# Normalising attention once per query tile: the softmax sums of eight head groups packed on rows of one PSUM block

## The chip, the cores and the metric

The kernel runs on one core of one Trainium2 chip. Its time is the device time of one launch, in microseconds. The kernel before was timed in three runs: 1523.5, 1524.84 and 1529.5 us, median 1524.84 us. One further execution was recorded by the profiler; it took 1528.72 us, of which 1527.0 us lie between its first and its last instruction (the span).

## The reference

The input is `x` of shape 2 x 1024 x 1024 in fp32. One "macaron" block is applied: half a feed-forward step, attention, half a feed-forward step again, with the same feed-forward weights both times.

```
x = x + 0.5 * ffn(layernorm(x))
x = x + attn(layernorm(x))
x = x + 0.5 * ffn(layernorm(x))

ffn(x)  = x @ base_w.T + base_b + 2 * (top-2-of-8 gated LoRA, rank 16)
attn(x): q = x @ Wq (32 heads of 32), k, v = x @ Wk, x @ Wv (8 heads of 32), rotary embedding on q and k,
         att = q k^T / sqrt(32), causal; probs = softmax(att); ctx = probs @ v; out = ctx @ Wo
```

Four query heads share one key/value head. A *group* below is one key/value head with its four query heads; there are eight groups. What the change touches is the division by the sum in the softmax, after `probs @ v`.

## The kernel before

The 2048 rows are 16 query tiles of 128 rows, tiles 0 to 7 for the first sequence and 8 to 15 for the second. Each tile goes through four stages: `a1` (layernorm, first feed-forward), `a2` (q, k, v projections with rotary embedding), `c1` (output projection and third layernorm) and `c2` (second feed-forward). Between a2 and c1 lies the attention of the tile, in eight *units*, one per group. A large fp32 product is made of three fp16 matmuls, high x high, high x low and low x high, so each operand is kept as a high and a low part (`Split`, lines 297 to 326, with the two-buffer tile `hl` and the four-buffer tile `tt`).

A unit has two passes over the key blocks of its tile (1 to 8 blocks, since attention is causal; L is their number). `unit_s1` (lines 558 to 604) computes the scores with queries on the rows, and VectorE takes their maxima (line 590). The maxima are written into extra columns of the query tensor (lines 602 and 603), and a transposing DMA brings the queries back (`qt_load`, line 553). `unit_s2` (lines 704 to 725) computes the scores again, transposed, with keys on the rows; ScalarE takes the exponential (line 718). The result `p32` is multiplied with the values by `av_batch` (lines 639 to 675), in batches of at most four key blocks.

`av_batch` issues fp32 matmuls of 32 columns of weights, four of them side by side in the array, one for each query head of the group, so that head h lands on rows 32h to 32h+31 of the PSUM bank `av`. The first half of the bank, `av[:, 0]`, takes values times probabilities; the second half, `av[:, 1]`, takes a weight block of ones times the same probabilities (added in pairs by VectorE, line 636), which gives the softmax sum, repeated on the 32 rows of each head. After the last batch of a unit, these lines run, once per unit, 128 times in all:

```
nc.scalar.copy(o, av)                                   # line 664, ScalarE, 128x256
nc.vector.reciprocal(rc, rc)                            # line 666, VectorE, 128x128
nc.vector.tensor_tensor(o2, o[:, 0, :], rc, ALU.mult)   # line 671, VectorE
nc.scalar.copy(c.high(g), o2)                           # line 672, ScalarE, fp16 high part
nc.gpsimd.tensor_tensor(c.low(g), o2, c.high(g), ...)   # line 673, GpSimd, fp16 low part
```

`c.high(g)` and `c.low(g)` are blocks of the context tile `tt`, which is the stationary operand of c1: block g of the contraction of c1 is group g. There is one `av` bank (pool `p_av`, one buffer).

The order of the work is written out by hand: `plan` (line 870) gives for each step s the pieces of a1, a2, c1 and c2 that are run between the units of tile s, and `SEQS` (line 861) the exceptions. In most steps c1 of the tile before begins after three pieces of c2 and one of a2. Tile 8 (`LATE`) is attended last, after tile 15; in that last step c1 of tile 15 and c1 of tile 8 follow closely upon their attention. On top of that the Tile scheduler, with a timing model of its own, sets the order of the instructions on each engine. The DMAs go out from SP's queue in one order: weight streams (`ws<-wstr`, line 370), query transposes (line 553), layernorm transposes (line 314), key transposes (line 501), rows in and out. A DMA that waits on SP holds all that is behind it.

Of the kernel before, what the change touches and what calls it, by code (L numbers as in the profile page):

```python
# [9 lines left out]
FP = mybir.dt.float32  # L10
HP = mybir.dt.float16
I32 = mybir.dt.int32
AF = mybir.ActivationFunctionType
ALU = mybir.AluOpType
AX = mybir.AxisListType

B, T, D = 2, 1024, 1024
NH, NKV, DH, GRP = 32, 8, 32, 4
E, R = 8, 16
P = 128  # L20
KB = D // P
NT = B * T // P
TPB = T // P
# [16 lines left out]
def kernel(  # L40
# [16 lines left out]
    nc = tc.nc  # L57
# [3 lines left out]
    const = ctx.enter_context(tc.tile_pool(name="const", bufs=1))  # L61
# [4 lines left out]
    hlp = ctx.enter_context(tc.tile_pool(name="hl", bufs=2))  # L66
    tp = ctx.enter_context(tc.tile_pool(name="tp", bufs=4))
    dram = ctx.enter_context(tc.tile_pool(name="dram", bufs=1, space=bass.MemoryType.DRAM))
# [6 lines left out]
    p_av = ctx.enter_context(tc.tile_pool(name="p_av", bufs=1, space=bass.MemoryType.PSUM))  # L75
# [10 lines left out]
        out=cmask, in_=cmask, compare_op=ALU.is_ge, fill=-NEG, base=0,  # L86
# [6 lines left out]
        out=tri, in_=tri, compare_op=ALU.is_gt, fill=0.0, base=0,  # L93
# [3 lines left out]
    nc.gpsimd.memset(mhalf, -0.5)  # L97
    half = const.tile([P, 1], FP)
    nc.gpsimd.memset(half, 0.5)
    ones = const.tile([P, DH], FP)  # L100
    nc.gpsimd.memset(ones, 1.0)
    cosT = const.tile([P, TPB, DH // 2], FP)
    sinT = const.tile([P, TPB, DH], FP)
    bb = const.tile([P, D], FP)
# [192 lines left out]
    class Split:  # L297


        def __init__(self, n):  # L300
            self.hl = hlp.tile([P, 2 * D], HP, name="hl")
            self.tt = tp.tile([P, 2 * KB, P], HP, name="tt")
            self.n, self.done = n, 0
# [16 lines left out]
        def high(self, k):  # L320
            m = KB // self.n
            return self.tt[:, k // m * 2 * m + k % m, :]
# [163 lines left out]
    KT, VA, QS, CTX, CT = {}, {}, {}, {}, {}  # L486
# [119 lines left out]
    pend = deque()  # L606
    ready = {}
    avt = [None]

    class Context:  # L610


        def __init__(self):
            self.tt = tp.tile([P, 2 * KB, P], HP, name="tt")

        def high(self, k):
            return self.tt[:, k, :]
# [4 lines left out]
    pairs = {}  # L622

    def add_pairs(batch):

        t, g, L, us = batch
        key = (t, g, us[0][0])
        if key in pairs:
            return
        pairs[key] = []  # L630
        for i in range(0, len(us), 2):
            if i + 1 == len(us):
                pairs[key].append(us[i][1])
                continue
            sums = pp.tile([P, GRP, P], FP, name="pair", bufs=2)
            nc.vector.tensor_tensor(sums, us[i][1], us[i + 1][1], ALU.add)  # L636
            pairs[key].append(sums)

    def av_batch():

        add_pairs(pend[0])
        t, g, L, us = pend.popleft()
        if us[0][0] == 0:
            avt[0] = p_av.tile([P, 2, P], FP, name="av")
        av = avt[0]
        last = us[-1][0] == L - 1
        runs = [(0, VA[t - t % TPB + j][:, g, :], p32) for j, p32 in reversed(us)]
        runs += [(1, ones, sums) for sums in reversed(pairs.pop((t, g, us[0][0])))]
        prev = None
        for n, (i, w, p32) in enumerate(runs):  # L650
            for h in range(GRP):
                rows = slice(h * DH, (h + 1) * DH)
                with ExitStack() as st:
                    if prev is not None:
                        st.enter_context(tc.high_priority())
                        st.enter_context(tc.issue_after(prev.ins))
                    prev = nc.tensor.matmul(  # L657
                        av[rows, i, :], lhsT=w, rhs=p32[:, h, :],
                        start=(us[0][0] == 0 and n == 0), stop=(last and n == len(runs) - 1),
                        skip_group_check=True, tile_position=(0, h * DH),  # L660
                    )
        if last:
            o = pp.tile([P, 2, P], FP, name="o", bufs=2)
            nc.scalar.copy(o, av)  # L664
            rc = o[:, 1, :]
            nc.vector.reciprocal(rc, rc)  # L666
            if t not in CTX:
                CTX[t] = Context()
            c = CTX[t]
            o2 = pp.tile([P, P], FP, name="o2", bufs=1)  # L670
            nc.vector.tensor_tensor(o2, o[:, 0, :], rc, ALU.mult)
            nc.scalar.copy(c.high(g), o2)  # L672
            nc.gpsimd.tensor_tensor(c.low(g), o2, c.high(g), ALU.subtract)  # L673
            if g == NKV - 1:
                CT[t] = CTX.pop(t)

    def av_add(t, g, j, L, p32):

        if not pend or len(pend[-1][3]) == BATCH or pend[-1][0:2] != (t, g):
            pend.append((t, g, L, []))  # L680
        pend[-1][3].append((j, p32))
        after = 0
        while len(pend) > 1:
            after = sum(len(b[3]) for b in list(pend)[1:])
            add_pairs(pend[0])
            if after < SKEW:
                break
            av_batch()
# [38 lines left out]
    def stage_c1(t):  # L727
        while t not in CT:
            av_batch()
        tt = CT.pop(t)  # L730
        xt = xts[t]
        for n in range(2):
            ps = p_dense.tile([P, 512], FP, name="pd")
            yield from dense_streamed(ps, tt, 3 + n)
            c = bass.ts(n, 512)
            nc.vector.scalar_tensor_tensor(xt[:, c], ps, S["uo", n], xt[:, c], ALU.mult, ALU.add)
            if n == 0:
                yield True
        Ts["x3", t] = layernorm(xt)
        yield True  # L740
# [31 lines left out]
    for h in range(2):  # L772
        for src, c in ((a_in, slice(0, P)), (g_in, slice(P, P + E))):
            pin(
                nc.sync.dma_start(
                    out=agst[:, h, :, c],
                    in_=src[h * (D // 2) : (h + 1) * (D // 2), :].rearrange("(k p) n -> p k n", p=P),
# [57 lines left out]
    pp = ctx.enter_context(tc.tile_pool(name="pp", bufs=2, reuse_waits="tile"))  # L835
# [5 lines left out]
    def flush(_):  # L841
        while pend:
            av_batch()
        yield True
# [195 lines left out]
```

## Time and profile before

| What | us | Where it is read |
|---|---|---|
| median of three runs | 1524.84 | times |
| profiled execution | 1528.72 | times |
| span of that execution | 1527.0 | head of the page |
| TensorE matmul busy | 1404.1 (92%) | part 1 |
| VectorE busy | 1139.7 (75%) | part 1 |
| ScalarE busy | 755.5 (49%) | part 1 |
| GpSimd busy | 450.1 (29%) | part 1 |
| share of the chain that ended last: PE, DVE, DMA, ACT | 65%, 13%, 13%, 3% | part 4 |

The profile names engines PE (TensorE), DVE (VectorE), ACT (ScalarE), POOL (GpSimd) and SP (the queue that issues most DMAs). A row of a group gives the line, the engine, the operation, output and inputs with shapes and the count; after the first bar the total busy time in us and the mean of one in ns; after the second bar the time that the engine stood idle just before them, and what ended it. The matmuls are pipelined: one of 512 columns is shown as 0.38 us long, but they start 0.216 us apart, so busy time of PE is not work of PE. The chain of waits goes back from the last instruction, at each step to what released it.

### The profile page before, as it was taken

To read this page: it belongs to the slowest core of one execution; us is meant where nothing else is said; L and a number is where in the kernel's file an instruction comes from. 1 tells how busy PE (TensorE), PEld (TensorE's weight loads), DVE (VectorE), ACT (ScalarE), POOL (GpSimd) and SP (SyncE) were. 2 spreads that over 40 slices of the span, in tenths; PEclk is the share of its full clock that TensorE was granted. 3 is DMA by queue.
4 is the path that set the end of the run, shared out by engine and by line. 5 is a ranking of instruction groups with operands and counts; after the bars stand their busy time and mean duration, and the time that the engine had idled before them with its cause. 6 is when DMAs were issued, how large, how long until landed. Compare 5 with 4: busy or idle time off the path is not lost.

```text
span 1527.0 us, 35303 instructions
## 1 busy us (share of the span) xinstructions
PE 1404.1 (92%) x14548; PEld 783.4 (51%) x14548; DVE 1139.7 (75%) x2420; ACT 755.5 (49%) x1374; POOL 450.1 (29%) x665
## 2 busy tenths in 40 slices
PE   3686897989999999999999899999999999989998
PEld 2243444455555555555654445555555555556544
DVE  6877656686968879789764767886869788689753
ACT  7564334453545545456552434553545455556631
POOL 3443213432323233122121323332323232312231
PEclk9798999989999999999999999999999999999999
DMA  9957697658575581853646769857383853834651
GB/s 274 333 156 204 115 237 205 206 127 264 123 238 137 153 254 31 235 160 69 209 160 191 216 161 272 202 160 234 72 294 69 237 147 70 271 69 98 133 170 45
DMA packets 293075, 267.30 MB, mean 175 GB/s; under 512 B 258480, under 2 KB 261552, under 8 KB 272432
## 3 DMA queue, kind: packets, MB, share of 16 engines
q1 hardware_dynamic: 289360, 252.45, 60.5%
q10 hardware_dynamic: 3552, 12.58, 2.3%
q8 instruction: 114, 1.87, 0.5%
q14 instruction: 49, 0.40, 0.1%
HBM read 181.63 MB, written 20.45 MB: 132 GB/s over the span
## 4 chain that ended last, share of the span: by engine, by line
PE 65%; DVE 13%; DMA 13%; ACT 3%; issue 2%; POOL 1%; SPq 1%; DVEq 0%; ACTq 0%; POOLq 0%
PE pd L358 13%; PE pd L359 13%; PE pd L360 13%; PE av L657 10%; PE s L712 7%; PE s L573 6%; DMA ws<-wstr 6%; DMA qt<-qst 5%; DVE mx L590 3%; DVE pair L636 1%; DVE ws L195 1%; DMA tt<-hl 1%; DVE o L666 1%; ACT p L718 1%; DVE hl L311 1%
## 5 line engine op out<-in xcount | busy, mean ns | idle before, releaser
L718 ACT ACTIVATE p<-s,cs 128x512 f32<-128x512 f32 x576 | 382.3, 688 | 291.2 <-PE s L712 284.1
L590 DVE TENSOR_REDUCE mx<-s 128x4 f32<-128x512 f32 x480 | 313.6, 675 | 68.3 <-PE s L573 46.8
L358 PE MATMUL pd<-ws,tt 128*128 128x512 f16 x592 | 226.8, 383 | 20.9 <-DMA ws<-wstr 16.8
L636 DVE TENSOR_TENSOR pair<-p,p 128x512 f32<-128x512 f32 x256 | 185.6, 727 | 72.6 <-ACT p L718 34.8
L573 PE MATMUL s<-kts,qt 96*128 96x128 f16 x2304 | 217.0, 222 | 23.8 <-DMA qt<-qst 17.8
L359 PE MATMUL pd<-ws,tt 128*128 128x512 f16 x592 | 226.3, 382 | 0.0
L712 PE MATMUL s<-qt,kts 128*128 128x512 f16 x576 | 210.7, 386 | 16.4 <-DMA qt<-qst 11.6
L360 PE MATMUL pd<-ws,tt 128*128 128x512 f16 x592 | 225.4, 382 | 0.0
L573 PEld LDWEIGHTS <-qt 96*128 96x128 f16 x2304 | 165.5, 99 | 116.4 <-issue 30.4
L359 PEld LDWEIGHTS <-tt 128*128 128x128 f16 x1360 | 135.6, 100 | 141.9 <-issue 31.3
L358 PEld LDWEIGHTS <-tt 128*128 128x128 f16 x1360 | 135.6, 100 | 135.5 <-issue 16.7
L358 PE MATMUL pd<-wb,tt 128*128 128x512 f16 x512 | 199.0, 389 | 5.0 <-DVE xt L444 5.0
L360 PEld LDWEIGHTS <-tt 128*128 128x128 f16 x1360 | 135.3, 99 | 131.5 <-issue 10.2
L359 PE MATMUL pd<-wb,tt 128*128 128x512 f16 x512 | 198.0, 387 | 0.5 <-DVE wb L195 0.5
L360 PE MATMUL pd<-wb,tt 128*128 128x512 f16 x512 | 197.7, 386 | 0.0
L657 PE MATMUL av<-p,va 128*32 128x128 f32 x4608 | 166.8, 278 | 4.8 <-ACT o L664 2.5
L720 POOL TENSOR_SCALAR_AFFINE_SELECT p<-p 128x512 f32<-128x512 f32 x128 | 89.0, 698 | 274.7 <-ACT p L718 264.4
L673 POOL TENSOR_TENSOR tt<-o,tt 128x128 f16<-128x128 f32 x128 | 70.5, 551 | 279.6 <-ACT tt L672 279.3
L657 PEld LDWEIGHTS av<-p,va 128*32 128x32 f32 x4608 | 115.5, 110 | 68.3 <-issue 53.4
L666 DVE RECIPROCAL o<-o 128x128 f32<-128x128 f32 x128 | 120.6, 942 | 24.9 <-ACT o L664 24.9
L585 POOL TENSOR_SCALAR_AFFINE_SELECT sm<-sm 128x512 f32<-128x512 f32 x96 | 66.4, 692 | 203.9 <-ACT sm L584 202.1
L395 POOL TENSOR_TENSOR xt<-xt,bb 128x512 f32<-128x512 f32 x64 | 92.3, 1464 | 59.6 <-ACT xn L349 59.4
(177 smaller groups left out, 1808.2 us busy)
## 6 DMA issues: line engine op xcount, KB each, us to landing
ws<-wstr SPq DMA_DIRECT2D x148, 1024.0 KB, 5.9
wstr<-ws ACTq DMA_DIRECT2D x9, 1024.0 KB, 6.1
xt<-in_x_dram SPq DMA_DIRECT2D x16, 512.0 KB, 3.8
out_dram<-xt SPq DMA_DIRECT2D x15, 512.0 KB, 2.8
ws<-in_wb_dram SPq DMA_DIRECT2D x2, 1024.0 KB, 8.0
qst<-in_wb_dram SPq DMA_DIRECT2D x2, 1024.0 KB, 6.8
st<-in_wo_dram SPq DMA_DIRECT2D x2, 1024.0 KB, 10.0
kts<-in_wo_dram SPq DMA_DIRECT2D x2, 1024.0 KB, 12.0
```

Of the source, the lines that this page charges most:

```text
L358: nc.tensor.matmul(ps, lhsT=th, rhs=wh, start=(k == 0), stop=False)
L359: nc.tensor.matmul(ps, lhsT=th, rhs=wl, start=False, stop=False)
L360: nc.tensor.matmul(ps, lhsT=tl, rhs=wh, start=False, stop=(last and k == KB - 1))
L395: nc.gpsimd.tensor_tensor(xt[:, c], xt[:, c], bb[:, c], ALU.add)
L573: nc.tensor.matmul(ps[:, h, :], lhsT=q[0 : 3 * DH, h, :], rhs=KT[b0 + j][0 : 3 * DH, g, :], start=(not pem or h == 0), stop=not pem,)
L590: nc.vector.tensor_reduce(mx[:, odd, j, :], ps, AX.X, ALU.max)
L636: nc.vector.tensor_tensor(sums, us[i][1], us[i + 1][1], ALU.add)
L657: prev = nc.tensor.matmul(av[rows, i, :], lhsT=w, rhs=p32[:, h, :], start=(us[0][0] == 0 and n == 0), stop=(last and n == len(runs) - 1), ...
L666: nc.vector.reciprocal(rc, rc)
L712: ins = nc.tensor.matmul(ps.rearrange("p h k -> p (h k)"), lhsT=KT[b0 + j][:, g, :], rhs=q.rearrange("p h k -> p (h k)"), start=True, stop ...
L718: nc.scalar.activation(p32, ps, AF.Exp, scale=cs)
L720: nc.gpsimd.affine_select(out=p32, in_=p32, compare_op=ALU.is_ge, fill=0.0, base=0, pattern=[[0, GRP], [1, P]], channel_multiplier=-1,)
```

## The change

The weight block `ones` becomes `pick`: 39 columns, zero but for columns 7 and 15 to 38. A window of 32 columns that begins at column 7 - g has ones in column g (from column 7) and in columns 8 + g to 31. The sums of group g are so accumulated on row g of each head's 32 rows, and all eight groups could share one 128x128 block (the ones in the later columns put positive numbers on rows 8 and beyond, which are not used). The bank `av` now holds three blocks of values, for three groups, and one block of sums. It is copied out by ScalarE after groups 2, 5 and 7: the values without division into the memory of the context tile (`c.raw`, seen as fp32), the sums into `den0`, `den1`, `den2`. After group 7 `finish` runs, once per tile: VectorE adds the three blocks and takes one reciprocal, the ScalarE queue writes it to DRAM, four DMAs from SP's queue read it back, each repeating one head's eight rows on 32 partitions, into a tile taken from the two buffers `hl`; then VectorE multiplies in two halves of 512 columns, ScalarE makes the high part and GpSimd the low part, in two halves each.

```
-    ones = const.tile([P, DH], FP)
-    nc.gpsimd.memset(ones, 1.0)
+    pick = const.tile([P, NKV - 1 + DH], FP)
+    nc.gpsimd.memset(pick, 0.0)
+    nc.gpsimd.memset(pick[:, NKV - 1 : NKV], 1.0)
+    nc.gpsimd.memset(pick[:, 2 * NKV - 1 :], 1.0)
...
+    HG, SLOTS = NKV // 2, 3
     class Context:
         def __init__(self):
             self.tt = tp.tile([P, 2 * KB, P], HP, name="tt")
+            self.raw = self.tt.bitcast(FP).rearrange("p k c -> p (k c)")
+            self.raw = self.raw.rearrange("p (g c) -> p g c", c=P)
+            self.dens = []
+        def finish(self):
+            rc = pp.tile([P, P], FP, name="rc", bufs=1)
+            nc.vector.tensor_tensor(rc, self.dens[0], self.dens[1], ALU.add)
+            nc.vector.tensor_tensor(rc, rc, self.dens[2], ALU.add)
+            nc.vector.reciprocal(rc, rc)
+            flat = dram.tile([P, P], FP, name="rcd", bufs=2)
+            nc.scalar.dma_start(out=flat, in_=rc)
+            bc = hlp.tile([P, 2 * D], HP, name="hl").bitcast(FP).rearrange("p (g q) -> p g q", q=P)
+            rows = flat.rearrange("(h d) q -> h d q", h=GRP)[:, 0:NKV, :]
+            for h in range(GRP):
+                nc.sync.dma_start(
+                    out=bc[h * DH : (h + 1) * DH],
+                    in_=rows[h].rearrange("g q -> (g q)").partition_broadcast(DH),
+                )
+            for i in range(2):
+                g = slice(i * HG, (i + 1) * HG)
+                nc.vector.tensor_tensor(bc[:, g], self.raw[:, g], bc[:, g], ALU.mult)
+            for i in range(2):
+                g = slice(i * HG, (i + 1) * HG)
+                hi, lo = self.tt[:, i * HG : (i + 1) * HG], self.tt[:, KB + i * HG : KB + (i + 1) * HG]
+                nc.scalar.copy(hi, bc[:, g])
+                nc.gpsimd.tensor_tensor(lo, bc[:, g], hi, ALU.subtract)
...
-        if us[0][0] == 0:
-            avt[0] = p_av.tile([P, 2, P], FP, name="av")
+        first, last = us[0][0] == 0, us[-1][0] == L - 1
+        slot = g % SLOTS
+        if first and slot == 0:
+            avt[0] = p_av.tile([P, SLOTS + 1, P], FP, name="av")
...
-        runs += [(1, ones, sums) for sums in reversed(pairs.pop((t, g, us[0][0])))]
+        one = pick[:, NKV - 1 - g : NKV - 1 - g + DH]
+        runs += [(SLOTS, one, sums) for sums in reversed(pairs.pop((t, g, us[0][0])))]
...
-        if last:
-            o = pp.tile([P, 2, P], FP, name="o", bufs=2)
-            nc.scalar.copy(o, av)
-            rc = o[:, 1, :]
-            nc.vector.reciprocal(rc, rc)
-            o2 = pp.tile([P, P], FP, name="o2", bufs=1)
-            nc.vector.tensor_tensor(o2, o[:, 0, :], rc, ALU.mult)
-            nc.scalar.copy(c.high(g), o2)
-            nc.gpsimd.tensor_tensor(c.low(g), o2, c.high(g), ALU.subtract)
-            if g == NKV - 1:
-                CT[t] = CTX.pop(t)
+        if last and (slot == SLOTS - 1 or g == NKV - 1):
+            with tc.high_priority():
+                nc.scalar.copy(c.raw[:, g - slot : g + 1], av[:, 0 : slot + 1])
+                den = pp.tile([P, P], FP, name=f"den{len(c.dens)}", bufs=1)
+                nc.scalar.copy(den, av[:, SLOTS])
+                c.dens.append(den)
+        if last and g == NKV - 1:
+            c.finish()
+            CT[t] = CTX.pop(t)
```

More of the change, by code (lines that the diff above doesn't have):

```diff
@@ L642, in av_batch @@
         t, g, L, us = pend.popleft()
-        if us[0][0] == 0:
-            avt[0] = p_av.tile([P, 2, P], FP, name="av")
+        if t not in CTX:
+            CTX[t] = Context()
+        c = CTX[t]
+        first, last = us[0][0] == 0, us[-1][0] == L - 1
+        slot = g % SLOTS
+        if first and slot == 0:
+            avt[0] = p_av.tile([P, SLOTS + 1, P], FP, name="av")
         av = avt[0]
-        last = us[-1][0] == L - 1
-        runs = [(0, VA[t - t % TPB + j][:, g, :], p32) for j, p32 in reversed(us)]
-        runs += [(1, ones, sums) for sums in reversed(pairs.pop((t, g, us[0][0])))]
+        one = pick[:, NKV - 1 - g : NKV - 1 - g + DH]
+        runs = [(slot, VA[t - t % TPB + j][:, g, :], p32) for j, p32 in reversed(us)]
+        nv = len(runs)
+        runs += [(SLOTS, one, sums) for sums in reversed(pairs.pop((t, g, us[0][0])))]
         prev = None
@@ L658, in av_batch @@
                         av[rows, i, :], lhsT=w, rhs=p32[:, h, :],
-                        start=(us[0][0] == 0 and n == 0), stop=(last and n == len(runs) - 1),
+                        start=(first and slot == 0 and n == 0), stop=(last and n in (nv - 1, len(runs) - 1)),
                         skip_group_check=True, tile_position=(0, h * DH),
                     )
-        if last:
-            o = pp.tile([P, 2, P], FP, name="o", bufs=2)
-            nc.scalar.copy(o, av)
-            rc = o[:, 1, :]
[L666 to L669, printed above, removed]
-            o2 = pp.tile([P, P], FP, name="o2", bufs=1)
-            nc.vector.tensor_tensor(o2, o[:, 0, :], rc, ALU.mult)
-            nc.scalar.copy(c.high(g), o2)
-            nc.gpsimd.tensor_tensor(c.low(g), o2, c.high(g), ALU.subtract)
-            if g == NKV - 1:
-                CT[t] = CTX.pop(t)
+        if last and (slot == SLOTS - 1 or g == NKV - 1):
[7 more added lines that the diff above has]
+            CT[t] = CTX.pop(t)
     def av_add(t, g, j, L, p32):
```

## The prediction

> **What bounds the kernel now.** I read the page's busy shares and its chain first, then the rows that the change touches, then what TensorE waits for, then the last 70 us as a timeline.
>
> ```profile
> PE 1404.1 (92%) x14548; PEld 783.4 (51%) x14548; DVE 1139.7 (75%) x2420; ACT 755.5 (49%) x1374; POOL 450.1 (29%) x665
> ...
> PE 65%; DVE 13%; DMA 13%; ACT 3%; issue 2%; POOL 1%; SPq 1%; DVEq 0%; ACTq 0%; POOLq 0%
> ...
> L666 DVE RECIPROCAL o<-o 128x128 f32<-128x128 f32 x128 | 120.6, 942 | 24.9 <-ACT o L664 24.9
> ```
>
> TensorE is the bound: two thirds of the chain, DVE and DMA about one eighth each. The reciprocal is the one large row that shrinks: 128 calls of 942 ns, a tenth of DVE. Summing the chain's list in 20 us slices, L666 stands on it with 19.5 us (24 pieces) and its product L671 with 5.3 us (17 pieces): 24.8 us in all.
>
> ```profile
> PE s L573 <- DMA qt<-qst: 17.8, 10, 5.7
> PE pd L358 <- DMA ws<-wstr: 16.8, 15, 2.2
> PE s L712 <- DMA qt<-qst: 11.6, 12, 2.1
> ...
> PE pd L358 <- DMA tt<-hl: 6.1, 5, 2.1
> PE s L573 <- DVE mx L590: 5.7, 15, 0.9
> ...
> PE s L712 <- ACT p L718: 4.3, 11, 1.2
> ```
>
> These are TensorE's waits (total, times, longest). Waits for DMAs add up to 52.3 us. Waits for DVE or ACT in the attention are small: with `pair` 2.7, `o` L664 2.5 and `o` L671 0.5 they come to 15.7 us. DVE is near its limit only in stretches, such as this one in tiles 12 and 13 (five and six key blocks):
>
> ```profile
> 1150.00:1200.00 50.00, 49.89 (x620) 29.40 (x618) 46.77 (x96) 28.98 (x53) 14.56 (x21) 1.00 0.37 74
> ```
>
> DVE (third figure) is busy 46.77 of 50 us.
>
> **What goes and what comes, by engine.** DVE loses 128 x (942 + 341) ns = 164.2 us. It gains 32 adds of 128x128 at 341 (L671's form) = 10.9, 16 reciprocals = 15.1, 32 products of 128x512 at 727 (L636's form) = 23.3. Net -115 us. ACT loses 47.7 (L664) + 38.0 (L672). It gains 48 copies of values (373 for 256 columns, L664; about 480 for 384, between it and 584 for 512, L584), 48 of sums at 0.27 (L436's form) and 32 casts at 0.61 (L508): 21 + 13 + 20 = 54. Net -32 us. POOL loses 70.5 (L673) and gains 32 x 1.46 (L395, a 128x512 two-input operation) = 46.8. TensorE is unchanged: as many matmuls, `pick` has 32 columns like `ones`. DMA gains 16 x (64 KB + 4 x 128 KB) = 9.4 MB beside 267 MB. The first memsets are hidden behind the loads of the start, some 0.3 us on POOL if not.
>
> **What the relief is worth.** Between 0 (the next arrival in each place is as late) and 24.8 us (all that the removed work holds on the chain). I take 14 us: near the 15.7 us that TensorE waits for DVE and ACT, below it for the part that does not come from this work, with some of the query transposes' 29.4 us (they wait for DVE's maxima) on top.
>
> **The new path at the end of a tile.** The old one is short: in the last unit ACT copies at 1488.3, and GpSimd ends the low part at 1490.9, 2.6 us. Block g of c1 also needed only group g. Now c1's first block needs group 7 and all of `finish`: ACT's two copies 0.37 + 0.27; DVE 0.34 + 0.34 + 0.94; the write; the four reads; the first product 0.73, cast 0.61, low part 1.46. The write of 64 KB has no row; `out_dram` lands in 2.8 us for 512 KB and 2.0 for 256, so 1.4 on their line, 1.7 with smaller runs (ends 1.4 and 2.8). For the reads the nearest row is the one other broadcast to partitions:
>
> ```profile
> bb<-in_bias_dram SPq DMA_DIRECT2D x1, 512.0 KB, 4.9
> ```
>
> The same bytes, 4 KB repeated on 128 partitions, 4.9 us. [...] I take 4.5 from the first issue to the last landing. The path is then 0.64 + 1.62 + 1.7 + 4.5 + 0.73 + 0.61 + 1.46 = 11.3 us, with the turns in seven queues 12 us (9 to 16).
>
> What covers it is the TensorE work between the tile's last `av` matmul and c1's first. I counted it in the order in which the changed kernel's matmuls are issued, at 0.216 us for 512 columns, 0.056 for a score matmul and 0.03 for an `av` one, which are the timeline's spacings. Twelve tiles have 17 us or more, so nothing shows; were that cover gone, each would cost up to 12. Tile 14 has 10.9 (1 us shows, or none). Tile 9 has 7.1 (it was 0.9, with the short path). Tile 15 has 6.1. Tile 8 ends its attention 5.7 us after c1 of tile 15 begins, and 11.0 us of matmuls follow. TensorE issues in order, so what is queued behind the wait, c1 itself, a2 of tile 11 or c2 of the last tiles, stands too: 4.9 us at tile 9, 5.9 at tile 15, about 1 at tile 8, 1 at tile 14.
>
> A stall also costs clock:
>
> ```profile
> 1487.74 0.40 PE L657 MATMUL av<-p,ones 128*32 128x128 f32 x8
> 1489.69 0.59 PE L358 MATMUL pd<-ws,tt 128*128 128x512 f16 x1 [1.55 <-DMA ws<-wstr]
> 1490.07 0.63 PE L359 MATMUL pd<-ws,tt 128*128 128x512 f16 x1
> 1490.50 0.63 PE L360 MATMUL pd<-ws,tt 128*128 128x512 f16 x1
> ```
>
> After a wait of 1.55 us the next matmuls start 0.43 us apart until 1492.6, half speed, 1.5 us lost. [...] The row decides: 1.5 us for each of the two long stalls (3 us[...]), none for the short ones at tiles 8 and 14, which the row would put at up to 3 more. Exposed in all 4.9 + 5.9 + 1 + 1 + 3 = 15.8; the 0.5 that tile 9 waited before goes: 15 us.
>
> **SP's queue.** Each tile puts four reads there. The first waits until the write has landed, 1.7 us after ACT issues it, and with four issues (1.3) SP is held 3.0 us, 48 in all. Behind it stand query transposes, weight streams and layernorm transposes, for which TensorE waits. Priced at the share of the chain that runs through DMA and SP, 14%: 7 us. Ends: 0 (SP has idled for DVE anyway: its query transposes waited 206.8 us for L603) and 20 (every tile delays a needed stream by over 1 us).
>
> **Smaller terms.** The one `av` bank is now freed by two copies, 0.75 us instead of 0.37, 48 times instead of 128; TensorE waited 2.5 us for it before. +1 (0 to 18, if each is exposed). DVE's product waits for the reads, and maxima and pair sums stand behind it. By the order on DVE, 1 to 22 us of other work lie between the reciprocal and the product, mostly 6 or more (8 us at 75% busy) against about 7 us for write and reads; short of it are tiles 3, 7 and 11, some 4 us of idle DVE each, mostly not on the path: +2 (0 to 8). One `hl` buffer is lent for about 8 us per tile while the layernorm uses two; the transposes behind are needed a step later: 0.
>
> **Sum.** -14 + 15 + 7 + 1 + 2 = +11 us, on the profiled 1528.7 gives 1539.7 (span 1527.0 + 11 = 1538). The profiled run lies 3.9 above the median, so against 1524.84: 1536.
>
> **Rivals.** (a) *The relief decides; faster.* The place is DVE in the tiles with five to eight key blocks. If the whole 24.8 us come back and the queue term is nil, 1524.8 - 24.8 + 18 = 1518; with tile 9 also covered (-6), 1512. It decides as soon as relief exceeds the costs: with the costs at 25 it needs all of it, with SP at 0 it needs 18. For it: DVE at 94% above. Against: TensorE is 49.89 of 50 busy in the same window. (b) *No change.* The path is 9 us long, the two stalls shrink to 2 and 3 us: 1524.8 + 11 - 9 = 1527. For it: quick landings of small transfers; against: three engines' queues on the way. (c) *SP becomes the bound after each tile.* The queue term is 20 and the path 16 us: 1536 + 13 + 8 = 1557. For it: 52.3 us of waits for DMA already; against: SP's own idle time. That the change doesn't act as it says I leave out: the DVE rows must shrink.
>
> **Chances and range.** Faster by over 0.5% (below 1517, rival a) 0.24; within 0.5%, which is about what timing this kernel can tell (1517 to 1532.5, rival b and the weak end of mine) 0.21; slower 0.55, of it 0.42 mine and 0.13 rival c. Range 1511 to 1557: it keeps most of a and c; my own case alone is 1530 to 1546.
>
> **What would show it.** DVE busy near 1025 us, L666's successor at 16 calls. TensorE waits of 4 to 7 us for GpSimd's or ACT's part of the context before c1 of tiles 9 and 15, followed by 0.43 us spacing; none at the other tiles. Waits for `qt` and `ws` up by about 7 us. The prediction is wrong if waits for `mx`, `p` and `pair` fall by more than 20 us, if the reads land within 3 us, or if a wait for the `av` copies appears 48 times.

## The result, and the profile after

The changed kernel takes 1539.26 us (median of 14 runs; 1523.57 us for the kernel before, 14 runs): a ratio of 1.0095, with a 95% interval of 1.0068 to 1.0123, so some 14.5 us slower. Its profiled execution took 1544.15 us, 15.4 more than that of before, with a span of 1542.4 us.

The page's busy times, its chain by engines, and the row of the reciprocal:

```profile
PE 1410.2 (91%) x14548; PEld 785.9 (51%) x14548; DVE 1055.0 (68%) x2244; ACT 723.5 (47%) x1246; POOL 422.9 (27%) x571
...
PE 62%; DVE 14%; DMA 13%; issue 4%; ACT 2%; POOL 2%; SPq 2%; DVEq 0%; POOLq 0%; ACTq 0%
...
L628 DVE RECIPROCAL rc<-rc 128x128 f32<-128x128 f32 x16 | 15.2, 947 | 0.2
```

The reciprocal shrinks from 120.6 us to 15.2, VectorE's busy time by 84.7 us and ScalarE's by 32.0, and TensorE is the bound as before. In the chain the share of TensorE falls by three points, and VectorE's, "issue" and SP's each rise by one or two.

TensorE's waits after (total us, times, longest), beside the eight shown of before:

```profile
PE s L576 <- DMA qt<-qst: 15.2, 8, 7.9
PE pd L361 <- ACT tt L644: 13.3, 4, 5.3
PE s L744 <- DMA qt<-qst: 13.2, 5, 4.5
PE pd L361 <- DMA ws<-wstr: 12.1, 10, 2.9
...
PE s L744 <- ACT p L750: 7.7, 13, 3.5
PE av L694 <- DVE pair L667: 5.6, 5, 2.4
...
PE s L576 <- DVE mx L593: 3.3, 12, 0.5
...
PE pd L361 <- DMA tt<-hl: 2.0, 3, 0.9
```

The waits for the query transposes are 28.4 us in their two rows (29.4 before), those for weight streams 12.1 (16.8). New is `ACT tt L644`, TensorE at c1 waiting for the high part that ScalarE makes of the normalised values: 13.3 us in four tiles. The waits for exponentials (`ACT p`) and for pair sums grew from 4.3 to 7.7 and from 2.7 to 5.6.

VectorE's waits have this new row, the product in `finish` waiting for the four reads:

```profile
DVE hl L640 <- DMA hl<-rcd: 37.5, 14, 6.2
```

and ScalarE's this one, the cast of the high part waiting for that product:

```profile
ACT tt L644 <- DVE hl L640: 48.8, 16, 6.3
```

The two transfers of the round trip (the last figure is the median from issue to landing):

```profile
hl<-rcd SPq DMA_DIRECT2D x64, 128.0 KB, 2.7
rcd<-rc ACTq DMA_DIRECT2D x16, 64.0 KB, 2.0
```

The stretch of 50 us in which VectorE was busy 46.77 us before:

```profile
1150.00:1200.00 50.00, 49.65 (x611) 29.32 (x610) 43.02 (x89) 30.08 (x51) 18.99 (x22) 1.00 0.47 106
```

VectorE has 43.02 there now, and TensorE 49.65 where it had 49.89.

Where those two waits go is seen in the timeline of the changed kernel at the end of tile 3 (start, duration, engine, line; in brackets the idle time before and what ended it):

```profile
415.06 0.94 DVE L628 RECIPROCAL rc<-rc 128x128 f32<-128x128 f32 x1
...
416.03 0.33 ACTq L630 DMA_DIRECT2D rcd<-rc  x1
...
416.46 1.84 ACT L750 ACTIVATE p<-s,cs 128x512 f32<-128x512 f32 x3 [3.16 <-DVE rc L628]
...
419.62 1.72 SPq L634 DMA_DIRECT2D hl<-rcd  x4
...
420.89 0.38 PE L744 MATMUL s<-qt,kts 128*128 128x512 f16 x1
...
421.97 0.38 PE L445 MATMUL pd<-lbh,ll 128*128 128x512 f16 x1
...
423.88 1.29 DVE L640 TENSOR_TENSOR hl<-tt,hl 128x512 f32<-128x512 f32 x2 [5.96 <-DMA hl<-rcd]
424.61 0.62 ACT L644 CAST tt<-hl 128x512 f16<-128x512 f32 x1 [6.30 <-DVE hl L640]
425.10 0.69 DVE L667 TENSOR_TENSOR pair<-p,p 128x512 f32<-128x512 f32 x1
425.13 0.68 ACT L750 ACTIVATE p<-s,cs 128x512 f32<-128x512 f32 x1
...
425.87 0.59 PE L744 MATMUL s<-qt,kts 128*128 128x512 f16 x1 [3.52 <-ACT p L750]
...
426.50 0.59 PE L361 MATMUL pd<-ws,tt 128*128 128x512 f16 x1
426.87 0.63 PE L362 MATMUL pd<-ws,tt 128*128 128x512 f16 x1
427.30 0.63 PE L363 MATMUL pd<-ws,tt 128*128 128x512 f16 x1
```

The reciprocal ends at 416.0, the write goes out at 416.03, the reads at 419.62, after the write has landed. VectorE finds 1.9 us of other work and then stands 5.96 us before the product. Behind the product stands the pair sum (425.10), although the exponentials that it adds had ended by 418.30. ScalarE's cast waits for the product, and behind the cast, in ScalarE's order, stands the exponential (425.13), although its scores had ended by 421.27. The second-pass scores of TensorE at 425.87 wait for that exponential, 3.52 us, and then matmuls of 512 columns start 0.43 us apart in place of 0.216 until 431.1, 12 of them at this half speed: 12 x 0.216 = 2.6 us more. So one wait of 5.96 us on VectorE stands ahead of 6.1 us lost on TensorE.

### The profile page after: what moved, and what is told of

It is laid out like the page before. It is cut to its first block, busy times and chain, and to the rows that moved or that the text cites. A ratio compares the mean times of both kernels' runs of the same rounds, so it can differ in the third digit from the quotient of the medians.

```text
span 1542.4 us, 35022 instructions
## 1 busy us (share of the span) xinstructions
PE 1410.2 (91%) x14548; PEld 785.9 (51%) x14548; DVE 1055.0 (68%) x2244; ACT 723.5 (47%) x1246; POOL 422.9 (27%) x571
## 4 chain that ended last, share of the span: by engine, by line
PE 62%; DVE 14%; DMA 13%; issue 4%; ACT 2%; POOL 2%; SPq 2%; DVEq 0%; POOLq 0%; ACTq 0%
PE pd L361 13%; PE pd L362 13%; PE pd L363 12%; PE av L694 10%; PE s L576 6%; PE s L744 6%; DMA qt<-qst 4%; DVE mx L593 4%; DMA ws<-wstr 3%; DMA hl<-rcd 3%; DVE pair L667 2%; DMA rcd<-rc 2%; DMA tt<-hl 1%; DVE ws L198 1%; SPq L634 1%
## 5 line engine op out<-in xcount | busy, mean ns | idle before, releaser
L593 DVE TENSOR_REDUCE mx<-s 128x4 f32<-128x512 f32 x480 | 315.0, 682 | 97.2 <-PE s L576 63.6
L361 PE MATMUL pd<-ws,tt 128*128 128x512 f16 x592 | 229.9, 388 | 27.0 <-ACT tt L644 13.3
L667 DVE TENSOR_TENSOR pair<-p,p 128x512 f32<-128x512 f32 x256 | 190.7, 747 | 67.7 <-ACT p L750 25.2
L576 PE MATMUL s<-kts,qt 96*128 96x128 f16 x2304 | 215.6, 221 | 18.8 <-DMA qt<-qst 15.2
L744 PE MATMUL s<-qt,kts 128*128 128x512 f16 x576 | 212.8, 387 | 21.7 <-DMA qt<-qst 13.2
L362 PE MATMUL pd<-ws,tt 128*128 128x512 f16 x592 | 229.9, 388 | 0.0
L363 PE MATMUL pd<-ws,tt 128*128 128x512 f16 x592 | 228.2, 386 | 0.0
L363 PEld LDWEIGHTS <-tt 128*128 128x128 f16 x1360 | 135.8, 100 | 131.6 <-issue 14.3
L588 POOL TENSOR_SCALAR_AFFINE_SELECT sm<-sm 128x512 f32<-128x512 f32 x96 | 70.9, 738 | 195.7 <-ACT sm L587 187.7
L352 ACT ACTIVATE xn<-xt,nb,rs 128x1024 f32<-128x1024 f32 x48 | 59.5, 1239 | 71.2 <-DVE nb L347 58.7
L694 PE MATMUL av<-pair,pick 128*32 128x128 f32 x2048 | 87.1, 276 | 5.8 <-DVE pair L667 5.6
```

The lines of the kernel that those rows point to most:

```text
L361: nc.tensor.matmul(ps, lhsT=th, rhs=wh, start=(k == 0), stop=False)
L362: nc.tensor.matmul(ps, lhsT=th, rhs=wl, start=False, stop=False)
L363: nc.tensor.matmul(ps, lhsT=tl, rhs=wh, start=False, stop=(last and k == KB - 1))
L576: nc.tensor.matmul(ps[:, h, :], lhsT=q[0 : 3 * DH, h, :], rhs=KT[b0 + j][0 : 3 * DH, g, :], start=(not pem or h == 0), stop=not pem,)
L588: nc.gpsimd.affine_select(out=sm, in_=sm, compare_op=ALU.is_ge, fill=-3.0e38, base=0, pattern=[[0, GRP], [-1, P]], channel_multiplier=1,)
L593: nc.vector.tensor_reduce(mx[:, odd, j, :], ps, AX.X, ALU.max)
```

## The experiments

In the table "us" is the ratio less one, times the 1523.6 us of the kernel before. The next three columns are from the profiled run of each: how long VectorE's product waited for the reads, how long TensorE waited in all, and how many of its matmuls of 512 columns that the timeline shows singly (about 4,100 in each) lasted over 0.5 us, those that run at half speed.

| Kernel | ratio (95%) | us | product's wait | TensorE's waits | at half speed | span |
|---|---|---|---|---|---|---|
| before | 1 | 0 | none | 117.5 | 95 | 1527.0 |
| changed | 1.0095 (1.0068-1.0123) | +14.5 | 37.5 | 127.4 | 145 | 1542.4 |
| before_no_recip | 0.9769 (.9748-.9791) | -35.2 | none | 90.4 | 82 | 1484.3 |
| after_no_reads | 0.9841 (.9816-.9866) | -24.2 | 0 | 97.2 | 70 | 1493.8 |
| after_late_product | 1.0000 (.9985-1.0016) | 0 | 25.3 | 114.2 | 113 | 1519.9 |
| after_short_path_4_tiles | 1.0123 (1.0099-1.0146) | +18.7 | 34.4 | 126.7 | 112 | 1537.8 |
| after_late_and_short_4 | 0.9928 (.9900-.9955) | -11.0 | 15.2 | 109.7 | 106 | 1514.2 |
| after_late_and_short_7 | 0.9888 (.9868-.9909) | -17.1 | 7.1 | 104.7 | 74 | 1503.9 |
| after_reads_on_act | 1.0171 (1.0137-1.0205) | +26.1 | 40.7 | 131.3 | 149 | 1551.7 |
| after_late_reads_on_act | 1.0063 (1.0035-1.0091) | +9.6 | 21.9 | 126.9 | 110 | 1536.0 |
| after_reads_on_gpsimd | 1.0096 (1.0071-1.0120) | +14.6 | 43.8 | 121.0 | 94 | 1529.4 |
| after_spread_on_tensor | 1.0067 (1.0045-1.0089) | +10.2 | 0 | 101.3 | 83 | 1530.4 |
| after_spread_tensor_late_4 | 0.9925 (.9906-.9944) | -11.4 | 0 | 91.0 | 66 | 1508.2 |

before_pow_on_gpsimd, at 2.15 times the time, is told below. The last columns add up: take from the span TensorE's waits and 0.216 us for each matmul at half speed, and what remains is 1376 to 1389 us in every kernel with the same TensorE work (before 1389, changed 1384, no reads 1381, late with short path in seven 1383). The spans lie 67 us apart, these remainders 13, so most of what differs between these kernels is TensorE's waiting and the clock after it. The profiled runs are single executions, those of before and changed some 5 us above their medians; the times are judged by the ratios.

**What the relief is worth.** The kernel before, without the reciprocal; its product takes a constant block, so the softmax is not divided by its sums.

```
-            rc = o[:, 1, :]
-            nc.vector.reciprocal(rc, rc)
+            rc = bb[:, 0:P]
```

> The kernel before with the reciprocal of line 666 left out (the product takes a constant block in its place, so the context is not normalised): 128 x 942 ns = 120.6 us less on VectorE, nothing else changed. The forecast's theory: the relief of VectorE is worth about 14 us (0 to 19.5, what L666 holds on the chain), so about 1510 us. The rival, that TensorE is the bound everywhere and the relief is worth nothing: 1520 to 1527 us.

Measured: 1486.55 us, 35.2 us faster, well over twice the 14 us of the theory, with VectorE's busy time down by 99.2 us (1139.7 to 1040.5): 0.35 us for each us of VectorE. TensorE's waits for DMAs in this kernel:

```profile
PE s L573 <- DMA qt<-qst: 10.4, 6, 5.2
PE s L711 <- DMA qt<-qst: 5.8, 6, 1.6
PE pd L358 <- DMA ws<-wstr: 16.3, 11, 2.8
```

The weight streams are as before (16.3 for 16.8), the query transposes 16.2 us for 29.4. These 13.2 us are nearly as much as all that TensorE waits for VectorE and ScalarE by name in the attention there (15.7): the transposes start when VectorE's maxima are done (in the kernel before, SP stood 206.8 us ahead of them, waiting for line 603), so a DMA's name on a wait can hide VectorE.

**The round trip as a whole.** The changed kernel with the write, but without the four reads; the product takes a constant block `cb`, so nothing is normalised.

```
-            for h in range(GRP):
-                nc.sync.dma_start(out=bc[h * DH : (h + 1) * DH], in_=rows[h]...)
+            cb = cst.unsqueeze(1).to_broadcast([P, HG, P])
...
-                nc.vector.tensor_tensor(bc[:, g], self.raw[:, g], bc[:, g], ALU.mult)
+                nc.vector.tensor_tensor(bc[:, g], self.raw[:, g], cb, ALU.mult)
```

> The changed kernel without the four reads of the reciprocals (the product takes a constant block, so the context is not normalised); the write to DRAM stays, and every other instruction too. The forecast's theory: the loss is all in the way through DRAM (TensorE's four waits for the context, VectorE's 37.5 us of waiting for the reads, SP's 44 us of waiting for the write) and the relief remains: about 1510 us, TensorE's wait for the context under 2 us. The rival, that the packed bank, its two copies out and the wider products and casts cost it: 1530 us or more.

Measured: 1495.96 us, 24.2 us faster than before. This is the relief that the change could bring; what comes with the reads costs 38.7 us on top of it, which makes the +14.5. The edit takes away a little more than the transfers: the product no longer needs the sums either, and in ten of the 16 tiles the trace shows both of its halves ahead of the tile's reciprocal (tile 3: 409.47 and 412.04 against 415.09). The run with TensorE in place of DRAM, below, keeps that dependence, and puts what the edit adds in this way at about 3 us. The same 22 us of the timeline, around the end of tile 3, as one window (TensorE's busy time first, the granted clock third from the end), in the changed kernel

```profile
410.00:432.00 22.00, 18.11 (x148) 8.64 (x141) 13.72 (x20) 8.51 (x17) 7.62 (x8) 0.84 0.53 117
```

and without the reads

```profile
410.00:432.00 22.00, 21.02 (x229) 11.37 (x228) 16.05 (x28) 10.87 (x20) 7.11 (x9) 1.00 0.54 153
```

show TensorE busy 18.11 us at a clock of 0.84 against 21.02 at 1.00.

**Which part of the round trip: the tile's end, the queue or the product?** Three edits, each taking one away.

(1) The short path of before, unit by unit, in the four tiles in which TensorE waited at c1 (0, 8, 9 and 15):

```
+    OLD = {0, LATE, LATE + 1, NT - 1}
...
+        own = t in OLD
+        slot = 0 if own else g % SLOTS
...
+        if last and own:
...
+            nc.scalar.copy(o, av[:, 0, :])
...
+            nc.scalar.copy(rc, av[:, SLOTS, :])
+            nc.vector.reciprocal(rc, rc)
...
+            nc.vector.tensor_tensor(o2, o, rc, ALU.mult)
+            nc.scalar.copy(c.high(g), o2)
+            nc.gpsimd.tensor_tensor(c.low(g), o2, c.high(g), ALU.subtract)
```

> The changed kernel, but tiles 0, 8, 9 and 15, whose context TensorE waited for, are normalised unit by unit as before. The forecast's theory (the exposed ends of these tiles are the largest cost): the 13.3 us of waits and some 3 us of half clock go, a quarter of the relief (3.5 us) is given back, so about 1527 us. The rival, that the queues behind the reads in all tiles are the cost: 1536 us or more.

Measured: 1539.47 us, where the theory had 1527 and its rival 1536 or more. None of the four waits at c1 is left, and nothing is won. VectorE's row says why in part:

```profile
DVE hl L643 <- DMA hl<-rcd: 34.4, 12, 6.6
```

The four tiles had 13.2 of the changed kernel's 37.5 us, but in the twelve that keep the round trip the waits are 34.4 us where they had been 24.3; tiles 10 and 11 alone have 10.1 us for 3.7. In these two VectorE had less other work between reciprocal and product (6.5 us for 10.5, 2.0 for 3.2); why the order came out so stays open. VectorE's busy time is also 24.9 us longer here, so the edit does more than take away the waits at c1.

(2) The product, and with it the casts and low parts that use it, later: in tiles 2 to 6 and 10 to 14 behind the pair sums of the next tile's first units. The transfers and their queues are the same. In the trace the product stands behind more work in eight of these tiles (3 to 6 and 11 to 14; in tile 3, 5.9 us for 2.0).

```
+        def apply(self, after=None):
...
+                with ExitStack() as st:
+                    if after is not None:
+                        st.enter_context(tc.issue_after(after))
+                    nc.vector.tensor_tensor(bc[:, g], self.raw[:, g], bc[:, g], ALU.mult)
...
+        elif first and g == NKV_AT:    # NKV_AT = 1
+            apply_all(pair_ins[-1] if pair_ins else None)
```

> The changed kernel with the product, and so the casts, of tiles 2 to 6 and 10 to 14 put later on VectorE: behind the pair sums of the next tile's first units. VectorE's wait for the reads in these tiles (19.5 us of 37.5) should nearly go. The forecast's theory prices these waits at 2 us: 1537 us. The rival, that the maxima and pair sums held behind the product are what costs the time: 1525 to 1530 us.

Measured: 1521.55 us, 14.5 us less than the changed kernel by the ratios and below the 1525 to 1530 of the rival. VectorE's row

```profile
DVE hl L652 <- DMA hl<-rcd: 25.3, 10, 6.8
```

fell by 12.2 us. Of TensorE's waits those at c1 did not fall at all, those for exponentials and pair sums did:

```profile
PE pd L361 <- ACT tt L656: 13.3, 4, 6.0
...
PE s L769 <- ACT p L775: 3.7, 11, 1.0
...
PE av L715 <- DVE pair L688: 1.5, 3, 1.0
```

These two fell by 8.1 us, from 7.7 and 5.6, and the 32 fewer matmuls at half speed are worth 6.9 us at 0.216: 15.0 in all, for 14.5 measured. TensorE's waits for DMAs stayed (42.0 us, 42.5 in the changed kernel), and SP still waited 44.4 us for the landing of the writes (44.1). So the place of the product, with its casts, in the engines' orders is what costs these 14.5 us, not the tile's end or SP's queue.

(3) The reads from another queue, so that SP does not stand behind the write: ScalarE's, as below, once with the product where it was and once with it late; and GpSimd's, by the same edit.

```
-                nc.sync.dma_start(
+                nc.scalar.dma_start(
```

> The changed kernel with the four reads issued from ScalarE's queue, right behind the write, and not from SP's. SP is no longer held by them (44 us in the changed kernel), nor do the reads stand behind weight streams on SP; ScalarE waits for the write instead, about 2 us per tile. The forecast's theory (SP's queue costs 7 us): about 1532 us. A stronger form of it (reads that land late because of what SP has issued before them are what VectorE waits for): 1520 to 1527 us, with VectorE's wait for the reads well under 20 us. The rival (it is the round trip as such): 1537 us or more, the wait for the reads unchanged.

> The late product with the reads on ScalarE's queue. If what the late product leaves (25 us above the kernel without reads) is SP's queue and late landings: about 1510 us. If it is the exposed ends of four tiles: 1518 us or more.

> The four reads of each tile go out from GpSimd's queue in place of SP's; nothing else. SP no longer stands 44 us behind the landing of the write; GpSimd (28% busy) does, with its selects and low parts behind. Theory (the hold of SP costs nothing, the wait of VectorE's product does): that wait stays at 30 us or more and the time stays within 1534 to 1548. Rival (SP's hold is a large part of the loss): 1520 to 1530, with TensorE's waits for qt and ws down by 5 us or more.

Measured: 1550.35 and 1535.21 us on ScalarE's queue, 11.6 and 9.6 us more than with SP's (26.1 against 14.5, and 9.6 against 0); the first fits its rival, the second only the outcome of 1518 or more. ScalarE's own work now stands behind the reads, and so in part behind the landing of the write:

```profile
ACT lg L401 <- DMA hl<-rcd: 7.4, 1, 7.4
ACT p L750 <- DMA hl<-rcd: 4.2, 1, 4.2
ACT tt L701 <- DMA hl<-rcd: 2.6, 1, 2.6
```

and TensorE's waits for exponentials rise from 7.7 to 14.3 us, and from 3.7 to 13.2 in the late form. On GpSimd's queue, 1535.16 us: the ratio is that of the changed kernel to 0.0001. TensorE's waits there:

```profile
PE s L576 <- DMA qt<-qst: 13.8, 9, 7.6
PE pd L361 <- DMA ws<-wstr: 12.5, 11, 3.1
PE s L744 <- DMA qt<-qst: 11.1, 7, 3.7
PE av L694 <- DVE pair L667: 10.7, 10, 3.8
PE av L694 <- POOL p L752: 8.4, 7, 3.4
```

Those for transposes and weights are 37.4 us where the changed kernel has 40.5, those for pair sums and GpSimd's masked exponentials 19.1 for 11.0. GpSimd waited 23.0 us for the write in SP's place. So freeing SP gave nothing in the time that the hold of another queue did not take back. What SP's hold costs is not shown by this: TensorE's waits for DMAs are 42.5 us in the changed kernel, 38.9 with the reads on GpSimd's queue, 35.9 on ScalarE's, and 34.7 without reads.

**The two together.** Late product, with the short path in tiles 0, 8, 9 and 15:

> The late product together with the unit-by-unit normalisation of tiles 0, 8, 9 and 15. If TensorE's 13.3 us of waits for the context in those four tiles count in full, with the half clock behind two of them: 16 us less than the late product alone, and some 8 us back for VectorE's additional work (29 us at the price that the kernel before without the reciprocal shows, 0.3 us per us): about 1513 us. If the ends do not count: 1522 us or more.

Measured: 1510.51 us, 11.0 us faster than before, near the 1513 for ends that count. The product's wait:

```profile
DVE hl L655 <- DMA hl<-rcd: 15.2, 7, 3.7
```

Then the three tiles in which it had still waited longest (1, 7 and 10; 9.4 us) on the short path too, seven in all:

```
-    OLD = {0, LATE, LATE + 1, NT - 1}
+    OLD = {0, 1, LATE - 1, LATE, LATE + 1, LATE + 2, NT - 1}
```

> The late product, with the short path in seven tiles (0, 1, 7, 8, 9, 10, 15) in place of four: the three added are those where the product waited longest, 3.4, 2.3 and 3.7 us. Theory: 9.4 us of waits go at 1 to 1.5 us each, and three tiles of relief at 25.5/16 = 1.6 us each are given back: 1510.5 - 9 to 14 + 5 = 1502 to 1506. Rival (a late product already hides these waits): 1511 to 1516.

Measured: 1505.39 us, within the theory's 1502 to 1506, 17.1 us faster than before with an interval of 0.9868 to 0.9909, and the fastest of all in which nothing is left out. Only

```profile
DVE hl L655 <- DMA hl<-rcd: 7.1, 3, 3.1
```

is left, although VectorE is busy 1090.5 us, 35.5 more than in the changed kernel.

**The round trip without DRAM.** TensorE spreads the reciprocals, in all tiles, and then in the late form with the short path in four:

```
-            nc.scalar.dma_start(out=flat, in_=rc)
...
+                ps = p_s1.tile([P, GRP, P], FP, name="s1")
+                for k in range(HG):
+                    for h in range(GRP):
+                        r = h * DH + i * HG + k
+                        nc.tensor.matmul(
+                            ps[h * DH : (h + 1) * DH, k, :],
+                            lhsT=ident[:, r : r + 1].to_broadcast([P, DH]), rhs=rc, ...)
+                nc.vector.tensor_tensor(bc[:, g], self.raw[:, g], ps, ALU.mult)
```

> The write to DRAM and the four reads are left out; the reciprocals of a tile are spread over the rows by TensorE instead: 32 matmuls per tile, each with one column of the identity repeated 32 times as weights, into two banks of the scores' pool, from which VectorE's product reads. Same result as the changed kernel. Theory (the wait of VectorE's product for the round trip is the largest cost): that wait is gone, and what is paid is 512 small matmuls at the av spacing of 0.03 us, 15 us; with the 1496 us of the kernel without reads some 1511, 1503 to 1520. Rival (the cost lies in the single, late normalisation of a whole tile, whatever way the reciprocals take): above 1530, with c1 of tiles 8 and 15 still waiting 2 to 5 us for ScalarE's high part.

> As the run with the late product and the short path in tiles 0, 8, 9 and 15 (1510.5 us), with TensorE in place of DRAM for spreading the reciprocals in the other twelve tiles; matmuls and product stand behind the pair sums of the next tile's first units. Theory: 15.2 us of VectorE's waits for the reads go, 384 small matmuls at 0.03 us (12 us) come, and half of the waits come back as waits for TensorE: 1505, 1498 to 1512. Rival: TensorE, at 92%, pays the 12 us and a wait for the reciprocal in its own queue: 1515 to 1525.

Measured: 1532.01 and 1509.97 us. The first was to be 1511, or above 1530 if the DRAM round trip were not the cause, and by the time alone the rival has it. The trace says otherwise. One tile's matmuls on the timeline (the 32 fp32 matmuls are recorded as 64):

```profile
941.82 1.93 PE L641 MATMUL s<-rc,ident 128*32 128x128 f32 x64
```

take 1.93 to 1.95 us, twice what I had put; at 1.95 that is 31.2 us in 16 tiles. The product now waits for TensorE in place of the reads, but 8.3 us in all, and TensorE's waits at c1 for ScalarE, which the rival wanted back at 2 to 5 us, are gone. All its waits and half-speed matmuls come to 101.3 + 83 x 0.216 = 119.2 us, against 158.7 in the changed kernel and 112.3 without reads, and the rest of the span is 1411 us in place of 1381 to 1384: about the matmuls' own 31.2 us. So the round trip's stalls were gone, and TensorE, the bound, paid for it in work. With the 31.2 us taken off its +10.2 the run stands 21.0 us below the kernel before, an estimate, and 3.2 short of the run without reads. With 12 tiles and the product late (23.4 us of matmuls) the time is in the theory's range, and the same exchange comes out even with the four-tile form.

**A different way to relieve VectorE.** The kernel before, with the reciprocal on GpSimd as a power of -1:

```
-            nc.vector.reciprocal(rc, rc)
+            nc.gpsimd.tensor_tensor(rc, rc, mone.to_broadcast([P, P]), ALU.pow)
```

> The kernel before with the reciprocal of line 666 taken on GpSimd (power of -1) and nothing else changed: the same 120.6 us leave VectorE without any way through DRAM. If GpSimd takes under 1.5 us for one, it has the room (450 us busy of 1527): 1490 to 1500 us, between the kernel without the reciprocal and the kernel before. If it takes over 3 us, GpSimd holds the masks behind it and the time is 1530 us or more.

Measured: 3281.86 us. GpSimd's row:

```profile
L668 POOL TENSOR_TENSOR o<-o,mone 128x128 f32<-128x128 f32 x128 | 2661.4, 20793 | 23.2 <-ACT o L666 23.2
```

One block took 20.8 us, 22 times VectorE's 0.942 us, and GpSimd was busy 94% of the span.

## Why the prediction was right or wrong

The forecast of 1536 us (1530 to 1546 for its own case) lies 3 us below the measured 1539.26, and "slower" was right. But two of the terms behind it were far off, and their errors largely offset each other: that the sum came out was luck.

**Relief, -14.** It was 24.2 us (without the reads; about 21 by the run with TensorE in place of DRAM), near the top end of 0 to 24.8 that I had from the chain. I had taken the 15.7 us that TensorE waits for VectorE and ScalarE by name as the measure, and only some of the transposes' 29.4. The transposes and streams were the larger part: without reads TensorE's waits for DMAs are 34.7 us, against 52.3 before.

**VectorE's product waiting for the reads, +2 (0 to 8).** This is the step that failed. I had 4 us of idle VectorE in three tiles, "mostly not on the path". It waited in 14 tiles, 37.5 us, and the part of it that the late product takes away, 12.2 us, cost 14.5 us of time, beyond the end of 8. The work between reciprocal and product was 5.6 us in the median tile (I had put mostly 6 or more), but the product started 8.2 us after the reciprocal's end in the median (I had about 7 for write and reads), and 13.1 at tile 8, where the reads went out behind three weight streams and it started 11.5 us after the first of the reads was issued. And I followed the wait only to the maxima and pair sums behind it on VectorE, not to ScalarE, where the cast waits for the product and exponentials stand behind the cast (tile 3 above).

The loss against the relief is 14.5 + 24.2 = 38.7 us. The edits, one upon the other, split it so: late product 14.5, short path in four tiles 11.0, in three more 6.1, and 7.1 us remain. In another order the shares differ (the short path alone in the four tiles gave nothing), and each tile on the short path also puts work back on VectorE. That 38.7 lies near the 37.5 us of the product's wait is no proof that all of it was this wait.

**Exposed tile ends, +15.** As waits the size was right, 13.3 us for 12.8, but the places were not:

```profile
213.36 0.61 PE L361 MATMUL pd<-ws,tt 128*128 128x512 f16 x1 [4.12 <-ACT tt L644]
...
954.34 0.39 PE L361 MATMUL pd<-ws,tt 128*128 128x512 f16 x1 [1.66 <-ACT tt L644]
...
1475.18 0.39 PE L361 MATMUL pd<-ws,tt 128*128 128x512 f16 x1 [2.15 <-ACT tt L644]
...
1499.73 0.61 PE L361 MATMUL pd<-ws,tt 128*128 128x512 f16 x1 [5.34 <-ACT tt L644]
1500.13 0.63 PE L362 MATMUL pd<-ws,tt 128*128 128x512 f16 x1
```

These are tiles 0 (none was forecast), 9 (1.66 us for 4.9), 15 (2.15 for 5.9) and 8 (5.34 for about 1). At tile 8 VectorE's product had itself waited 6.22 us, so much of this is the same stall seen further down, and taking it away alone gave nothing; with the product late it gave 11.0 us, along with 10.1 us of the product's waits. So in these tiles it was hardly a term to be added beside that wait. The clock was undersized: 3 us for two stalls, where 22 matmuls at half speed follow three of these four, 4.8 us at 0.216. In the whole kernel it is 50 more than before, 10.8 us, 12 of them behind the stall of tile 3. The two last lines start 0.40 us apart, and those that follow 0.43. Half speed came at once after waits of 4.12 and 5.34 us, and also after the 1.55 us that the prediction showed; after 1.66 us it did not come, and after 2.15 us at tile 15 seven half-speed matmuls are shown, from 0.7 us later on. So in these traces the length of a wait alone does not tell whether half speed follows.

**SP's queue, +7.** Open. SP waited 44.1 us for the writes (48 forecast). The sign that I had named, waits for transposes and weights up by 7 us, did not come: against before they fell by 5.7. But before is the wrong measure, since the relief alone lowers such waits. Against the run without reads TensorE's waits for DMAs are 7.8 us longer (42.5 for 34.7), of the size forecast, and SP's order is plain at two of the exposed ends: the reads of tile 0 went out 18.1 us after its write had landed, those of tile 8 behind three weight streams. With the product late they hardly change (42.0), which speaks against their being the product's wait seen again. No run frees SP alone, without taking the round trip away or holding another engine's queue, so none shows what this cost in time.

**The av bank, +1.** The row of TensorE waiting for the copy of `av` (2.5 us before) is gone: 0.

**Durations.** Write 2.0 us (1.7 forecast), reads 2.7 each and 5.0 in the median from the first issue to the last landing of a tile's four (4.5 forecast, my estimate beside the 4.9 of the one broadcast that the page before shows), product 0.69 (0.73), cast 0.615 (0.61), low part 1.30 (1.46). VectorE's busy time fell by 84.7 us, not 115: removed and added rows come to -117.5 us by their sums. Some other rows grew, all rows together fell by 104.2 (1261.9 to 1157.7), and the rows add up to more than the busy time (1139.7), because neighbours overlap (in tile 3 the pair sum runs from 425.10 to 425.79, the next instruction from 425.70) and the sum counts the overlap twice; with fewer instructions less of it was there to go (122.2 us before, 102.7 after).

**The rivals.** (a), the relief decides, had the relief nearly right (24.2 of 24.8) and fell with the product's wait. (b) wanted small stalls, which the 37.5 us speak against. (c) wanted 20 us from SP's queue, where TensorE's waits for DMAs rose by 7.8 against the run without reads.

## What to carry to other kernels

Before an instruction is put behind a DMA round trip, count the work that its engine has between the issue of the transfer and the data, and follow what is queued behind it through every engine that waits for it (in tile 3 the pair sum started 6.8 us after its exponentials had ended, behind the waiting product); here the engine waited 37.5 us in this way, and moving the instruction behind the next independent work gave 14.5 us of time back with the transfers untouched. Where only the last places have no such work, keep the short path there, as the kernel at 1505.39 us does. A wait named for a DMA can be a busy engine's that released the DMA late (13.2 of the 29.4 us of waits for query transposes went with the reciprocal), so price the relief of an engine from the waits for both.

## What was not expected of the hardware

A power of -1 on GpSimd took 20.8 us for 128x128 in fp32. An fp32 matmul of 32 weight columns and 128 data columns took 0.061 us of TensorE's time (1.95 us for 32), so 32 of them per tile were not small change. And a stall can cost TensorE more than its length: after 3.52 us of waiting in tile 3 the next 5.2 us ran at half speed, so 74% were added to it; after 1.66 us at tile 9 nothing was.
